# A graph layer on one core: 62 row tiles for 58, ScalarE's addresses at column 64, and the first receivers' copy behind the table's last write

## The chip, the cores and the metric

The kernel runs on one core of one Trainium2 chip. The metric is the device time of one execution in microseconds (us), as the median over runs. The engines are named as in the profile: PE is TensorE, DVE is VectorE, ACT is ScalarE, POOL is GpSimd and SP is SyncE; ACTq and SPq are the instruction queues of ScalarE and SyncE, which also issue DMA transfers, and PEld is TensorE's loading of weights.

## The reference

One layer of a graph network: 6250 nodes with 128 features, 206250 edges sorted by receiver. For each edge two small networks give a weight vector, the sender's key and value are fetched, and a weighted sum goes to the receiver; a residual and a layer norm follow.

```python
w_ij = silu(edge_feats @ rad_W1 + rad_b1) @ rad_W2 + rad_b2
w_ij = w_ij + silu(chi_scalar @ sph_W1 + sph_b1) @ sph_W2 + sph_b2
q_i = (x @ Wq).reshape(-1, 8, 16)[receivers]
k_j = (x @ Wk).reshape(-1, 8, 16)[senders]
alpha = (q_i * w_ij.reshape(-1, 8, 16) * k_j).sum(-1) / sqrt(16) * cutoffs[:, None]
v_j = (x @ Wv)[senders].reshape(-1, 8, 16)
out = segment_sum(alpha[..., None] * v_j, receivers) / 16
return layernorm(x + out.reshape(-1, 128))
```

## The kernel before

**Tiles.** Edges are cut into 403 *quads* of 512 edges (four tiles of 128, one edge a partition), four quads to a *group*, two groups to a pair. The list `order` holds the quads in the sequence of processing. The loop runs over groups g and four slots; i counts its passes, and pass i multiplies quad i+1, while activations are made one quad further ahead.

**Table phase (up to about 57 us).** The node features come in by 13 chunks. TensorE turns each chunk and multiplies it with Wk and Wv (L392), VectorE copies the product out (L394), and SyncE writes it to the table `kv_tab` in DRAM (L399): one row of 1 KB, key and value, for each node. The first 8 quads get their keys and values from gathered node features by the same matmuls instead of from the table (`gather_x`, tile `msg`). Beside this the receivers of each edge, relative to a group's first node, are turned (L472), written to DRAM as `rel_lin` (L480), copied within DRAM to `rel_pair`, repeated four times (L488), and read back as `relb` (L272), from which VectorE makes the one-hot matrices `hotT` (L301). For the first group this is `first_rel`, which stands beside chunk 7; for all others it is `store_rel(1, PAIRS)` behind the table phase. SyncE's queue runs in order, so what stands behind a waiting DMA there waits too.

**Gathers.** From quad 8 on, keys and values come from `kv_tab`. GpSimd issues one indirect DMA for each 128 edges (L141), 14 quads ahead of their use, into a ring of 16 buffers. The first of them needs the whole table written.

**Row tiles.** In some quads the last of the four tiles is not gathered by GpSimd. Its 128 rows are fetched by 128 plain DMAs of 1 KB (L210) into `wide`, issued by SyncE and ScalarE. ROW_TILES is their number, spread evenly over passes 8 to 401; ROW_ACT is the number of rows of each that ScalarE issues, the others are SyncE's. An address has to stand in a register of the issuing engine, and loads from the tile `at_i` put it there (L204, TENSOR_LOAD): 32 registers at a time on SyncE and 24 on ScalarE (ROW_UNITS). `at_i` is made once, by VectorE's copies of a turned list (L811 and L812). How many rows an engine issues in a pass is dealt out by `load_rows` from the pass number; a load counts as six rows. ScalarE issues one row at each of two places between its activations and the rest at the end of the pass.

**A quad's arithmetic.** First layers on TensorE (L566), SiLU on ScalarE (L603, two a quad), second layers (L618), queries at edges (L585); VectorE multiplies by the keys (L634, which waits for the gathers and rows in its queue at L631) and by the weights (L642), sums by head (L644), scales (L647) and forms messages (L659); TensorE sums the messages with one-hot matrices (L670, L711). SiLU of a quad waits for a mark of TensorE, and TensorE's first layers wait for SiLU to free one of two PSUM banks.

## Time and profile before

| | |
|---|---|
| median of 3 runs | 1966.89 us (1962.34 to 1968.69) |
| the profiled execution | 1962.43 us, span 1960.5 us |
| mean granted TensorE clock | 0.955 |
| gathers of keys and values on GpSimd (L141) | 1522 |
| rows issued by ScalarE and SyncE (L210) | 4176 and 3248 |
| loads of addresses, ScalarE and SyncE (L204) | 174 and 116 |
| busy share of the DMA engines in most slices | 0.5 |

In the profile's rows a number of partitions and elements stands behind the tile names, "x" is a count, and "|" parts busy time and mean from the idle time before the group and what ended it. In the answers by source line, min/median/max of the duration in ns follow the count, then the first and the last start in us. In the order of time, a row begins with start and length in us. Windows give busy us and counts of PE, PEld, DVE, ACT and POOL, then the granted clock, the share of the DMA engines and GB/s.

### The profile page before, as it was taken

The numbers are of one execution on the slowest core, as the hardware profiler recorded it, in microseconds if no ns is written. First come the engines' busy times: TensorE is split into PE (matmuls) and PEld (weight loads), VectorE is DVE, ScalarE is ACT, GpSimd is POOL, SyncE is SP. The second block draws the span as 40 slices with busy tenths as digits, with TensorE's granted clock in tenths as the row PEclk, the third lists the DMA queues.
The fourth block names the chain that finished last, engine by engine and source line by source line (L and its number), as shares of the span: only waits on it lengthen the run. The fifth ranks groups of instructions, "written<-read, shape, count | busy, mean of one in ns | idle before, by whom it ended". The sixth has DMA issues, their size and how long they took to land.

```text
span 1960.5 us, 55953 instructions
## 1 busy us (share of the span) xinstructions
PE 1785.3 (91%) x16005; PEld 1498.5 (76%) x16005; DVE 1521.0 (78%) x3366; ACT 644.3 (33%) x1361; POOL 1471.3 (75%) x1562
## 2 busy tenths in 40 slices
PE   9999999998999999888988899989899898988888
PEld 7777777777877777777877777777777777777777
DVE  6787888778887787777777777877777777777778
ACT  3333333332333333333333333333333333323234
POOL 7777777777777777777777777777777777777775
PEclk9999999998999999989989999999899999999999
DMA  9755555555555555555545554555555555545543
GB/s 324 222 144 147 166 145 164 152 145 150 166 144 151 168 145 149 165 143 152 168 142 146 161 155 144 147 168 145 145 150 166 143 145 161 155 142 148 163 133 99
DMA packets 148925, 307.13 MB, mean 157 GB/s; under 512 B 40326, under 2 KB 76608, under 8 KB 148608
## 3 DMA queue, kind: packets, MB, share of 16 engines
q0 software_dynamic: 74080, 201.69, 36.8%
q1 hardware_dynamic: 64400, 96.98, 15.2%
q10 hardware_dynamic: 10128, 4.82, 1.2%
q8 instruction: 127, 2.08, 0.4%
q14 instruction: 190, 1.56, 0.3%
HBM read 289.88 MB, written 15.11 MB: 156 GB/s over the span
## 4 chain that ended last, share of the span: by engine, by line
ACTq 24%; POOL 16%; DMA 16%; DVE 14%; issue 13%; PE 10%; ACT 3%; POOLq 0%; DVEq 0%
ACTq L210 19%; POOL kv L141 16%; DMA kv<-kv_tab,src_i 16%; ACTq L204 5%; PE pw L618 4%; DVE kq L634 3%; DVE side L644 2%; PE pq L585 2%; DVE kq L642 2%; ACT act L603 2%; DVE msg L659 2%; PE ph L566 2%; PE po L670 1%; DVE side L647 1%; PE pq L711 0%
## 5 line engine op out<-in xcount | busy, mean ns | idle before, releaser
L141 POOL DMA_INDIRECT kv<-kv_tab,src_i x1522 | 1439.7, 946 | 465.5 <-issue 395.4
L603 ACT ACTIVATE act<-ph,b 128x512 f32<-128x512 f32 x806 | 554.5, 689 | 1265.6 <-issue 752.0
L618 PE MATMUL pw<-w,act 128*128 128x128 f32 x6448 | 875.0, 292 | 0.0
L618 PEld LDWEIGHTS pw<-w,act 128*128 128x128 f32 x6448 | 796.3, 201 | 52.8 <-issue 7.7
L566 PE MATMUL ph<-feats,w 32*128 32x512 f32 x1612 | 600.0, 665 | 54.3 <-ACT act L603 51.5
L634 DVE TENSOR_TENSOR kq<-pq,kv 128x512 f32<-128x512 f32 (+1 forms) x404 | 270.6, 670 | 358.3 <-DVEq L631 197.3
L585 PE MATMUL pq<-q,hotT 32*128 32x128 f32 x3224 | 490.0, 292 | 5.9 <-DVE kq L634 5.8
L585 PEld LDWEIGHTS pq<-q,hotT 32*128 32x128 f32 x3224 | 408.6, 193 | 26.0 <-DVE kq L634 21.3
L566 PEld LDWEIGHTS ph<-feats,w 32*128 32x128 f32 x1612 | 180.6, 188 | 206.2 <-ACT act L603 149.9
L644 DVE TENSOR_REDUCE side<-kq 128x32 f32<-128x512 f32 x404 | 280.3, 694 | 14.0
L659 DVE TENSOR_TENSOR msg<-kv,side 128x512 f32<-128x512 f32 (+1 forms) x404 | 269.1, 666 | 13.9
L642 DVE TENSOR_TENSOR kq<-pw,kq 128x512 f32<-128x512 f32 x404 | 274.6, 680 | 0.0
L573 PE MATMUL pw<-brow,onesb 3*128 3x512 bf16 x403 | 158.2, 393 | 0.0
L670 PE MATMUL po<-msg,hot 128*32 128x128 f32 x3200 | 153.6, 289 | 0.0
L711 PE MATMUL pq<-part,to 128*128 128x128 f32 x196 | 45.2, 314 | 77.5 <-DVE kq L634 77.5
L670 PEld LDWEIGHTS po<-msg,hot 128*32 128x32 f32 x3200 | 71.1, 110 | 37.9 <-issue 3.8
L711 PEld LDWEIGHTS pq<-part,to 128*128 128x128 f32 x196 | 31.1, 200 | 87.5 <-DVE kq L634 79.2
L647 DVE TENSOR_TENSOR side<-side,scale 128x32 f32<-128x32 f32 x400 | 79.8, 199 | 13.7
L301 DVE TENSOR_TENSOR hotT<-relb,side 128x512 f32<-128x512 bf16 x101 | 68.7, 681 | 1.5 <-DMA relb<-rel_pair 1.5
L306 DVE TENSOR_TENSOR hot<-rel,side 128x512 f32<-128x512 f32 x100 | 68.0, 680 | 0.0
L295 PE MATMUL pq<-wq,xT 128*128 128x128 f32 x200 | 43.0, 298 | 25.9 <-DVE kq L634 25.7
L295 PEld LDWEIGHTS pq<-wq,xT 128*128 128x128 f32 x200 | 31.0, 195 | 31.8 <-DVE kq L634 28.0
(133 smaller groups left out, 824.9 us busy)
## 6 DMA issues: line engine op xcount, KB each, us to landing
wide<-kv_tab ACTq DMA_DIRECT2D x4176, 1.0 KB
wide<-kv_tab SPq DMA_DIRECT2D x3248, 1.0 KB
feats<-in_edges SPq DMA_DIRECT2D x50, 1024.0 KB
kv<-kv_tab,src_i POOLq DMA_INDIRECT x1522, 3.2
relb<-rel_pair SPq DMA_DIRECT2D x50, 256.0 KB
x<-in_x SPq DMA_DIRECT2D x101, 64.0 KB
out<-y SPq DMA_DIRECT2D x101, 64.0 KB
kv_tab<-kv SPq DMA_DIRECT2D x12, 512.0 KB
```

The source lines that it names most:

```text
L141: return nc.gpsimd.indirect_dma_start(out=o, out_offset=None, in_=table, in_offset=bass.IndirectOffsetOnAxis(ap=index, axis=0))
L210: o = engine.dma_start(row_of[q][p:p + 1, 0, :].bitcast(U8), table[:, ds(regs.pop(p), ROW_BYTES)])
L566: return nc.tensor.matmul(act_of[q, i], w1[r0:r0 + R, :], feats_of[g][r0:r0 + R, c0:c0 + EQ], start=True, stop=True)
L573: nc.tensor.matmul(pw, onesb[f:f + 3, :], brow[f:f + 3].rearrange("p t d -> p (t d)"), start=True, stop=False)
L585: o = nc.tensor.matmul(pq_of[q][:, t, :], hotT_of[g][b, t * P:(t + 1) * P], q_of[g][b, :], start=True, stop=True)
L603: o = nc.scalar.activation(act, act_of[q, i], AF.Silu, bias=b1[:, i:i + 1])
L618: o = nc.tensor.matmul(pw[:, t, :], act_of[q, i][:, t * P:(t + 1) * P], w2[:, i, :], start=False, stop=(t == QT - 1 and i == 1))
L634: o = nc.vector.tensor_tensor(kq_of[q][:, u, :], pq_of[q][:, u, :], kv[:, :, :D], op=OP.mult)
L642: nc.vector.tensor_tensor(m, pw_of[q][:, t, :], m, op=OP.mult)
L644: nc.vector.tensor_reduce(alpha, m.rearrange("p t (h e) -> p t h e", e=HD), AX.X, OP.add)
L659: nc.vector.tensor_tensor(msg_of[q][:, u, :].rearrange("p t (h e) -> p t h e", e=HD), kv[:, :, D:].rearrange("p t (h e) -> p t h e", e=HD) ...
L670: o = nc.tensor.matmul(po_of[g][j * W:(j + 1) * W, :], hot_of[g][:, j * QT + t, :], msg_of[g * NQ + j][:, t, :], start=(t == 0), stop=(t = ...
```

## The change

The number of row tiles goes from 58 to 62. In each, ScalarE issues 70 rows instead of 72 and SyncE 58 instead of 56. In `at_i` the addresses no longer stand at their row's number: SyncE's begin at column 0 and ScalarE's at column 64, so the tile is 144 columns wide and VectorE fills it with four copies instead of two. Further, the copy from `rel_lin` to `rel_pair` becomes a function of its own, `store_pairs`; for the first group it is called behind the last write of `kv_tab`, in the last chunk's pass, no longer beside chunk 7. For the other groups it stays directly behind `store_rel`.

```diff
--- before.py
+++ after.py
@@ -49,11 +49,12 @@
 MSGS = 10
 ACTS = 8
 RING = 16
-ROW_TILES = 58
+ROW_TILES = 62
 ROW_FIRST = 8
 ROW_LAST = 401
 ROW_LEAD = 6
-ROW_ACT = 72
+ROW_ACT = 70
+ROW_AT = {SP: 0, ACT: 64}
 ROW_LOAD = 6
 ROW_CARRY = 2
 ROW_UNITS = {SP: 32, ACT: 24}
@@ -201,8 +202,9 @@
             regs = {}
 
             def load(e, m):
+                c = ROW_AT[name] + e - a
                 regs.update(zip(range(e, e + m), nc.values_load_multi_w_load_instructions(
-                    at_i[q % P:q % P + 1, q // P, e:e + m], engines=(name,), min_val=0,
+                    at_i[q % P:q % P + 1, q // P, c:c + m], engines=(name,), min_val=0,
                     max_val=(N - 1) * ROW_BYTES,
                     skip_runtime_bounds_check_because="senders are nodes")[1]))
 
@@ -480,6 +482,9 @@
                     nc.sync.dma_start(
                         rel_lin[h, u:e:NQ].rearrange("n m e -> m n e"),
                         relT[p:p + GT, u // NQ:u // NQ + n, :])
+        def store_pairs(c, d):
+
+            ends_at = [min(d, (NG + 1 - h) // 2) for h in range(2)]
             for h, e in enumerate(ends_at):
                 r = rel_lin[h].rearrange("u (j t) e -> (u j) (t e)", t=QT)
                 m = e - (e - c) % NQ
@@ -544,6 +549,7 @@
             for f in beside.get(k, []):
                 f()
             if i == len(chunks) - 1:
+                store_pairs(0, 1)
                 load_rel(0, gp, 1)
                 load_feats(0)
                 for g in range(1, XL):
@@ -554,6 +560,7 @@
             gathers(q, mark_of[quads_x[n + 2 + (n > 1)], "x"] if n else None)
         nc.vector.tensor_tensor(bsum, b2[:, 0:1], b2[:, 1:2], op=OP.add)
         store_rel(1, PAIRS)
+        store_pairs(1, PAIRS)
         nc.vector.tensor_scalar(scale, scale, SCALE, None, op0=OP.mult)
 
 
@@ -800,7 +807,7 @@
             nc.vector.tensor_scalar(general, found, 0.0, None, op0=OP.is_gt)
 
         rows_f = quad_of("kq", 3).rearrange("p t d -> p (t d)")[:, :QUADS]
-        at_i = lp.tile([P, math.ceil(QUADS / P), P], I32, name="at_i")
+        at_i = lp.tile([P, math.ceil(QUADS / P), ROW_AT[ACT] + 80], I32, name="at_i")
 
         def turn_rows():
             pt = pp.tile([P, EQ], F32, name="pq", bufs=2).rearrange("p (t d) -> p t d", d=P)
@@ -808,8 +815,10 @@
             for i in range(full + 1):
                 n = min(P, QUADS - i * P)
                 nc.tensor.transpose(pt[:n, i, :], rows_f[:, i * P:i * P + n], ident)
-            nc.vector.tensor_copy(at_i[:, :full, :], pt[:, :full, :])
-            nc.vector.tensor_copy(at_i[:n, full, :], pt[:n, full, :])
+            m = P - ROW_ACT
+            for a, b, at in ((0, m, ROW_AT[SP]), (m, P, ROW_AT[ACT])):
+                nc.vector.tensor_copy(at_i[:, :full, at:at + b - a], pt[:, :full, a:b])
+                nc.vector.tensor_copy(at_i[:n, full, at:at + b - a], pt[:n, full, a:b])
 
         written, ready, ready_at = [], [], []
         load_rel(1, lp, 2)
```

The change moves lines, so the listings of the changed program below have L482, L493, L401, L274, L258 for L480, L488, L399, L272, L256, and L212, L206, L610, L292, L722 for L210, L204, L603, L290, L715. On SyncE, at the end of the table phase, where the last writes of the table and the first group's receivers meet, this stands before:

```order
L399 DMA kv_tab<-kv 128x1024
L480 DMA rel_lin<-relT 16x128 x2
L488 DMA rel_pair<-rel_lin 16x1x512 x2
L399 DMA kv_tab<-kv 128x1024 x4
L399 DMA kv_tab<-kv 128x256
L272 DMA relb<-rel_pair 128x1x1024
L256 DMA feats<-in_edges 128x2x1024
```

and this with the change:

```order
L401 DMA kv_tab<-kv 128x1024
L482 DMA rel_lin<-relT 16x128 x2
L401 DMA kv_tab<-kv 128x1024 x4
L401 DMA kv_tab<-kv 128x256
L493 DMA rel_pair<-rel_lin 16x1x512 x2
L274 DMA relb<-rel_pair 128x1x1024
L258 DMA feats<-in_edges 128x2x1024
```

The two copies to `rel_pair` have moved behind the five last table writes and stand directly ahead of the load of `relb` that reads them; the load of `feats` still follows that.

On ScalarE, in the third and fourth pass with rows, between activations (`act`, `xT`, `tot`), before:

```order
L603 ACTIVATE act_102<-ph,b_72 128x512
L210 DMA wide<-kv_tab 1x1024
L290 ACTIVATE xT<-pq 128x128
L603 ACTIVATE act_103<-ph,b_72 128x512
L210 DMA wide<-kv_tab 1x1024 x11
L603 ACTIVATE act_104<-ph,b_72 128x512
L210 DMA wide<-kv_tab 1x1024
L715 ACTIVATE tot<-pq 128x128
L210 DMA wide<-kv_tab 1x1024
L603 ACTIVATE act_105<-ph,b_72 128x512
L210 DMA wide<-kv_tab 1x1024 x10
L204 TENSOR_LOAD at_i
```

and with the change, about the same place:

```order
L292 ACTIVATE xT<-pq 128x128
L212 DMA wide<-kv_tab 1x1024
L610 ACTIVATE act_103<-ph,b_72 128x512
L212 DMA wide<-kv_tab 1x1024 x12
L610 ACTIVATE act_104<-ph,b_72 128x512
L212 DMA wide<-kv_tab 1x1024
L722 ACTIVATE tot<-pq 128x128
L212 DMA wide<-kv_tab 1x1024
L610 ACTIVATE act_105<-ph,b_72 128x512
L212 DMA wide<-kv_tab 1x1024 x4
L206 TENSOR_LOAD at_i
```

A stretch between two quads' activations now takes 12 rows where it took 10 or 11, and the loads come after fewer quads.

On VectorE the four casts that fill `at_i` stand where two stood, between the first quad's message and the second quad's multiply, and the four new row tiles split eight operations in two. TensorE's sequence is the same, and GpSimd issues 1518 gathers instead of 1522.

## The prediction

> **What bounds the kernel now.** I read the page first, then GpSimd's order of time, then counts by line in windows, then ScalarE's queue.
>
> ```profile
> PE 1785.3 (91%) x16005; PEld 1498.5 (76%) x16005; DVE 1521.0 (78%) x3366; ACT 644.3 (33%) x1361; POOL 1471.3 (75%) x1562
> L141 POOL DMA_INDIRECT kv<-kv_tab,src_i x1522 | 1439.7, 946 | 465.5 <-issue 395.4
> ...
> 44.45 0.94 POOL L141 DMA_INDIRECT kv<-kv_tab,src_i  x1 [1.42 <-DVE kv L394]
> 45.70 0.95 POOL L141 DMA_INDIRECT kv<-kv_tab,src_i  x1 [0.30 <-issue]
> ...
> 1947.23 0.95 POOL L141 DMA_INDIRECT kv<-kv_tab,src_i  x1 [0.30 <-issue]
> ```
>
> TensorE has the largest share, yet GpSimd is the engine without a pause. From the first gather's start to the last one's there are 1521 steps in 1902.8 us, 1.251 us each, and a neighbouring pair shows the same step: 0.95 busy and 0.30 to issue. A quad takes four gathers, one fewer where a row tile replaces one, so with 58 tiles over 393 quads GpSimd's pace is (4 - 58/393) x 1.251 = 4.819 us a quad.
>
> That sets the end only while someone waits for it. I count gathers issued (L141) and first multiplies started (L634, one a quad) up to four moments:
>
> ```profile
> L141 POOL DMA_INDIRECT kv<-kv_tab,src_i x45: 942/946/1221, 44.4 to 99.8; - x45
> L634 DVE TENSOR_TENSOR kq<-pq,kv x10: 668/692/693, 59.2 to 98.7; 128x512 f32<-128x512 f32 x10
> ...
> L141 POOL DMA_INDIRECT kv<-kv_tab,src_i x276: 942/946/1221, 44.4 to 388.8; - x138
> L634 DVE TENSOR_TENSOR kq<-pq,kv x73: 550/692/693, 59.2 to 384.6; 128x512 f32<-128x512 f32 x64, 128x384 f32<-128x384 f32 x9
> ...
> L141 POOL DMA_INDIRECT kv<-kv_tab,src_i x556: 942/946/1221, 44.4 to 739.0; - x186
> L634 DVE TENSOR_TENSOR kq<-pq,kv x150: 549/692/693, 59.2 to 738.9; 128x512 f32<-128x512 f32 x130, 128x384 f32<-128x384 f32 x20
> ...
> L141 POOL DMA_INDIRECT kv<-kv_tab,src_i x1484: 942/946/1221, 44.4 to 1899.7; - x186
> L634 DVE TENSOR_TENSOR kq<-pq,kv x391: 547/692/694, 59.2 to 1895.0; 128x512 f32<-128x512 f32 x168, 128x384 f32<-128x384 f32 x28
> ```
>
> The first 8 quads need no gather and a row quad needs three. At 100 us ten multiplies have used 8 gathers of 45: 37 are ahead. At 390 it is 276 - (65 x 4 - 9) = 25, at 740 it is 556 - (142 x 4 - 20) = 8, at 1900 again 1484 - (383 x 4 - 56) = 8. So there are two regimes: until about 740 the arithmetic runs faster than GpSimd and eats its head start of 29 gathers (36.3 us); after that it waits for each gather to land. The waits agree: in 100 to 390 us VectorE's multiply waits for TensorE, in 850 to 1900 for its own queue's wait on the landings.
>
> ```profile
> DVE kq L634 <- PE pq L585: 45.1, 48, 2.3
> ...
> DVE kq L634 <- DVEq L631: 180.8, 119, 3.9
> ```
>
> What sets the pace of the first regime? ScalarE's engine is only a third busy, but its queue also issues row transfers. Here are 100 to 390 us (L603 twice a quad), then ten row issues in a stretch:
>
> ```profile
> L603 ACT ACTIVATE act<-ph,b x128: 682/688/692, 100.8 to 388.5; 128x512 f32<-128x512 f32 x128
> L210 ACTq DMA_DIRECT2D wide<-kv_tab x678: 227/228/538, 100.8 to 389.7; - x170
> L204 ACTq TENSOR_LOAD <-at_i x29: 1707/1810/1954, 98.7 to 385.8; - x29
> ...
> 105.69 3.10 ACTq L210 DMA_DIRECT2D wide<-kv_tab  x10
> ...
> PEld ph L566 <- ACT act L603: 44.5, 82, 1.9
> ```
>
> 64 quads in 290 us are 4.53 us a quad. A row costs (3.10 - 0.23)/9 = 0.32 us of the queue, a load 1.81 and about 0.06 around it. 678 rows and 29 loads make 217 + 54 = 271 of the 290 us; the 19 left are 0.3 us a quad for dispatching activations. The queue is full, and TensorE's weight loads wait for its SiLUs. So the first regime is bound by ScalarE's instruction queue, at 4.53 us a quad.
>
> **The change part by part.** *Four gathers fewer.* 4 x 1.251 = 5.0 us off GpSimd; its pace becomes (4 - 62/393) x 1.251 = 4.807.
>
> *The receivers' copy moved.* The startup on SyncE and its two readers:
>
> ```profile
> 29.23 1.66 SPq L480 DMA_DIRECT2D rel_lin<-relT  x2
> 34.04 1.48 SPq L488 DMA_DIRECT2D rel_pair<-rel_lin  x2
> 35.61 4.26 SPq L399 DMA_DIRECT2D kv_tab<-kv  x5
> 39.97 1.36 SPq L272 DMA_DIRECT2D relb<-rel_pair  x1
> ...
> 45.48 0.69 DVE L301 TENSOR_TENSOR hotT<-relb,side 128x512 f32<-128x512 bf16 x1 [1.52 <-DMA relb<-rel_pair]
> ```
>
> The copy waits 3.1 us (30.89 to 34.04) for its input to land, with five table writes queued behind. Without it the last write is issued about 2 us earlier, when its data is ready. The first gather then starts up to 1.42 - 0.30 = 1.1 us earlier; GpSimd's gathers of x keep it from more. I take 1.1 (bounds 0 and 1.1). Now the relb load, with feats, x and scale behind it, waits for the copy: issue about 37.8 to 39.3, plus a landing like those 3.1 us, so relb leaves at 42.4 instead of 39.97. VectorE already idles 1.52 us for it and the table-phase copies stand behind. Compute starts 0 to 2.4 us later; I take 2, since the wait is exposed.
>
> *More rows on ScalarE.* Rows per quad go from 58 x 72/393 = 10.63 to 62 x 70/393 = 11.04: +0.42 x 0.32 = 0.133 us. Loads go from 174/393 to 186/393: +0.03 x 1.87 = 0.057. Every third load fetches 22 registers instead of 24; SyncE's loads of 24 and 32 registers span
>
> ```profile
> L204 SPq TENSOR_LOAD <-at_i x116: 1673/1960/2302, 73.5 to 1902.0; - x116
> ```
>
> so at most 0.08 us a register, -0.02 a quad. What starting at column 64 does for a load is unshown. It lies between all loads at the fastest (1.71 instead of 1.81: -0.05 a quad) and at the slowest (1.95: +0.07). ScalarE's loads began at three columns (56, 80, 104) and hardly vary, so I take 0. The queue needs 4.53 + 0.133 + 0.057 - 0.02 = 4.70 us a quad, bounds 4.65 to 4.77.
>
> *More on the others.* SyncE gets 348 rows (111 us) and 8 loads, covered by 332 us that it waits for marks of TensorE; uncovered, rows would come late and add to VectorE's L631 wait.
>
> ```profile
> SPq L324 <- PE pq L585: 218.4, 73, 10.1
> SPq L256 <- PE pq L585: 113.9, 45, 4.6
> ```
>
> VectorE gets two small casts once and eight operations split in two (550 + 281 ns for 692), under its 22% of idle time; uncovered, some 2 us.
>
> ```profile
> L634 DVE TENSOR_TENSOR kq<-pq,wide 128x128 f32<-128x128 f32 x58 | 16.3, 281 | 0.0
> ```
>
> *Clock.* The quiet pace is not the mean. Windows 100 to 390, 390 to 500, 500 to 740, 850 to 1900, with granted clock after the counts:
>
> ```profile
> 100.00:390.00 290.00, 269.65 (x2483) 221.20 (x2483) 232.77 (x513) 97.51 (x205) 219.24 (x232) 1.00 0.53 154
> 390.00:500.00 110.00, 100.81 (x916) 86.33 (x914) 90.19 (x204) 35.40 (x75) 83.19 (x88) 0.91 0.53 153
> 500.00:740.00 240.00, 226.20 (x2067) 186.27 (x2067) 194.78 (x435) 82.03 (x173) 181.59 (x192) 0.99 0.53 152
> 850.00:1900.00 1050.00, 947.21 (x8566) 799.19 (x8565) 802.00 (x1770) 338.47 (x716) 793.75 (x841) 0.94 0.53 152
> ...
> L603 ACT ACTIVATE act<-ph,b x46: 682/688/694, 390.9 to 496.8; 128x512 f32<-128x512 f32 x46
> ```
>
> At 0.91 a quad took 110/23 = 4.78 us, 0.25 more. From 100 to 740 the clock was 0.98 and 140 quads took 4.573 each, 0.04 over the quiet pace. A slower ScalarE leaves TensorE idle more often, so I take 0.06: compute at 4.76 us a quad, bounds 4.74 (that mean) and 4.87 (clock 0.94 throughout: 0.06/0.09 x 0.25 = 0.17).
>
> *The sum.* The head start to lose is 36.3 + 1.1 (earlier gathers) + 2 (later compute) + 2 (0.17 us on some 12 quads before 100 us) = 41.4 us. The last 8 quads carry no rows and run faster:
>
> ```profile
> 1930.37 0.69 DVE L634 TENSOR_TENSOR kq<-pq,kv 128x512 f32<-128x512 f32 x1
> 1934.38 0.68 DVE L634 TENSOR_TENSOR kq<-pq,kv 128x512 f32<-128x512 f32 x1
> 1937.86 0.68 DVE L634 TENSOR_TENSOR kq<-pq,kv 128x512 f32<-128x512 f32 x1
> 1941.59 0.69 DVE L634 TENSOR_TENSOR kq<-pq,kv 128x512 f32<-128x512 f32 x1
> ```
>
> that is 3.74 each, and win 8 x 1.07 = 8.5. The other 33 must be lost over 384 quads, 0.086 a quad, so compute has to do 4.72 to catch GpSimd. At 4.76 it wins 384 x 0.047 = 18 and ends 15 us behind. GpSimd's own end moves by -5.0 - 1.1 = -6.1. Sum: +9 us on the span 1960.5, on this execution's 1962.43 (1.9 us lie outside the span): 1971. The median of the runs, 1966.89, is 4.5 above that execution; I forecast 1976.
>
> **The rivals.** *A: compute still catches up and GpSimd sets the end.* Then it is 6.1 us faster, 1961. For it: quiet compute at 4.70 is under 4.72. Against: that margin is 0.02, half of what the clock already cost before 740 us.
>
> *B: the clock falls and stays low.* TensorE idles in more stretches, runs them at half rate, and its late marks hold ScalarE back. At 4.87 compute loses 384 x 0.063 = 24 instead of winning: 33 + 24 - 6 = +51, 2018. For it: the window with most idle time (850 on, TensorE 90% busy) has 0.94. Against: 100 to 390 kept 1.00 at 93%. The Trainium skill, "TensorE: Matmul & The Clock Gate", Part 1, says that the clock goes to half after an idle window of about 3.4 us and returns after a busy one; the rows of lower clock where TensorE waits fit that, and by this rule alone the change tends towards B.
>
> *C: the copy gives back all it gains and nothing else moves.* If row issues hid in ScalarE's waits, rows would be free and the end would be -5 to -6, within noise of A. The full queue of 100 to 390 us speaks against it; I count it with A.
>
> **How the numbers follow.** A measurement tells about 0.3% (5.9 us) from no change. Compute-bound, 4.73 to 4.82 a quad (-2 to +32 us): 0.6, of it 0.48 above +5.9. A with C: 0.28, half of it beyond -5.9. B: 0.12. So faster 0.18, same 0.22, slower 0.60. The likeliest's own range is 1965 to 1999; with A it reaches down to 1960: 1960 to 1999.
>
> **What would show it.** The same count of gathers ahead should fall from some 38 at 100 us to clearly above 8 at the end, and the L634 wait on L631 should almost vanish. SiLU pairs should be 4.7 or more apart, relb's wait at L301 some 2 us longer, the first gather near 43.3. If the head start is gone by 1500 us, or ScalarE's loads are much shorter from column 64, the forecast is wrong on the fast side; a mean clock under 0.95 says B.

## The result and the profile after

| | before | after |
|---|---|---|
| median of the runs | 1967.07 us (1962.34 to 1968.69, 4 runs) | 2028.62 us (2025.04 to 2031.87, 4 runs) |
| span of the profiled execution | 1960.5 us | 2023.2 us |
| mean granted TensorE clock | 0.955 | 0.953 |

The changed kernel is slower: the ratio is 1.031, with a 95% interval of 1.0294 to 1.0326. The direction was forecast, the size was not: 9 us were forecast, 62 came.

Three parts of the changed kernel's profile: busy times, then the chain that ended last by engine and by line, then the gathers.

```profile
PE 1851.2 (91%) x16005; PEld 1525.8 (75%) x16005; DVE 1522.9 (75%) x3376; ACT 645.3 (32%) x1361; POOL 1471.5 (73%) x1558
...
ACTq 62%; issue 14%; PE 12%; ACT 7%; DVE 4%; DMA 0%; SPq 0%; DVEq 0%
ACTq L212 49%; ACTq L206 13%; ACT act L610 5%; PE pw L625 4%; PE ph L573 3%; PE pq L592 2%; PE pk L394 1%; DVE kq L641 1%; DVE side L651 1%; DVE kq L649 1%; PE po L677 1%; ACT y L753 1%; PE pt L384 0%; ACT q L299 0%; ACT part L713 0%
...
L142 POOL DMA_INDIRECT kv<-kv_tab,src_i x1518 | 1439.6, 948 | 471.9 <-issue 394.5
```

GpSimd's work is hardly changed, and nothing that GpSimd does is in the chain any more. ScalarE's queue alone makes 62% of it, 49% by row issues (L212) and 13% by loads of addresses (L206). Before, that chain was mixed:

```profile
ACTq 24%; POOL 16%; DMA 16%; DVE 14%; issue 13%; PE 10%; ACT 3%; POOLq 0%; DVEq 0%
```

The waits between 850 and 1900 us of the changed kernel (the stretch in which before's multiply waited for landed gathers, 180.8 us of it) agree:

```profile
ACT act L610 <- issue: 642.1, 189, 5.5
DVE kq L641 <- PE pq L592: 226.0, 180, 4.1
...
PEld ph L573 <- ACT act L610: 192.0, 315, 2.8
```

No wait of the multiply for a landing is left. TensorE waits for SiLUs, VectorE for TensorE, and a SiLU mostly for no other engine (71 us for TensorE stand against the 642): it stands behind row issues and loads in ScalarE's own queue. Now gathers issued (L142) and first multiplies (L641), as the prediction counted them, up to 100, 390, 740 and 1900 us:

```profile
L142 POOL DMA_INDIRECT kv<-kv_tab,src_i x44: 942/949/1440, 44.9 to 99.4; - x44
L641 DVE TENSOR_TENSOR kq<-pq,kv x9: 669/691/692, 60.8 to 95.6; 128x512 f32<-128x512 f32 x9
...
L142 POOL DMA_INDIRECT kv<-kv_tab,src_i x275: 942/949/1440, 44.9 to 388.8; - x138
L641 DVE TENSOR_TENSOR kq<-pq,kv x69: 550/692/693, 60.8 to 385.4; 128x512 f32<-128x512 f32 x60, 128x384 f32<-128x384 f32 x9
...
L142 POOL DMA_INDIRECT kv<-kv_tab,src_i x555: 942/949/1440, 44.9 to 739.9; - x185
L641 DVE TENSOR_TENSOR kq<-pq,kv x141: 546/692/693, 60.8 to 736.1; 128x512 f32<-128x512 f32 x121, 128x384 f32<-128x384 f32 x20
...
L142 POOL DMA_INDIRECT kv<-kv_tab,src_i x1475: 941/949/1440, 44.9 to 1900.0; - x185
L641 DVE TENSOR_TENSOR kq<-pq,kv x378: 545/692/693, 60.8 to 1896.0; 128x512 f32<-128x512 f32 x160, 128x384 f32<-128x384 f32 x29
```

Gathers ahead are 44 - 4 = 40 at 100 us, 275 - (61 x 4 - 9) = 40 at 390, 555 - (133 x 4 - 20) = 43 at 740 and 1475 - (370 x 4 - 58) = 53 at 1900. Before they fell from 37 to 8. The arithmetic never catches GpSimd; it falls further behind until GpSimd is held: 53 gathers at 3.84 a quad are about the 14 quads that it may run ahead.

From 100 to 1900 us before starts 391 - 10 = 381 multiplies, after 378 - 9 = 369: 1800/381 = 4.72 us a quad and 1800/369 = 4.88. Some 384 quads at 0.154 us more are 59 us, and the first multiply is 1.6 us later (60.8 for 59.2). Together that is 61 of the 62.7 us on the span.

To see what fills ScalarE's queue, I summed every record of it within a window and divided by the quads (half the number of L610 SiLUs). "Each" is the mean of a row's issue with the 29 ns move before it; "gaps" is the time between records, on the right the gaps in which a SiLU is dispatched, where waiting shows too.

```
us a quad           window    quad  rows   each   rows  loads  gaps  gaps at SiLUs
before              100-390   4.53  10.59  273 ns 2.89  0.79   0.64  0.19
before              850-1900  4.78  10.61  271 ns 2.88  0.80   0.64  0.47
after               100-390   4.83  11.00  276 ns 3.04  0.88   0.68  0.21
after               850-1900  4.90  11.07  281 ns 3.11  0.89   0.68  0.21
```

Before, the queue waits in the second stretch (0.47) and works through in the first (0.19). After, it works through everywhere.

### The profile page after: what moved, and what is told of

Same layout as the page of the kernel before. It is cut to its first block, busy times and chain, and to the rows that moved or that the text cites. A ratio compares the mean times of both kernels' runs of the same rounds, so it can differ in the third digit from the quotient of the medians.

```text
span 2023.2 us, 57021 instructions
## 1 busy us (share of the span) xinstructions
PE 1851.2 (91%) x16005; PEld 1525.8 (75%) x16005; DVE 1522.9 (75%) x3376; ACT 645.3 (32%) x1361; POOL 1471.5 (73%) x1558
## 4 chain that ended last, share of the span: by engine, by line
ACTq 62%; issue 14%; PE 12%; ACT 7%; DVE 4%; DMA 0%; SPq 0%; DVEq 0%
ACTq L212 49%; ACTq L206 13%; ACT act L610 5%; PE pw L625 4%; PE ph L573 3%; PE pq L592 2%; PE pk L394 1%; DVE kq L641 1%; DVE side L651 1%; DVE kq L649 1%; PE po L677 1%; ACT y L753 1%; PE pt L384 0%; ACT q L299 0%; ACT part L713 0%
## 5 line engine op out<-in xcount | busy, mean ns | idle before, releaser
L142 POOL DMA_INDIRECT kv<-kv_tab,src_i x1518 | 1439.6, 948 | 471.9 <-issue 394.5
L610 ACT ACTIVATE act<-ph,b 128x512 f32<-128x512 f32 x806 | 554.4, 689 | 1325.8 <-issue 1155.7
L625 PE MATMUL pw<-w,act 128*128 128x128 f32 x6448 | 892.3, 296 | 0.0
L625 PEld LDWEIGHTS pw<-w,act 128*128 128x128 f32 x6448 | 812.4, 205 | 52.0 <-issue 5.9
L573 PE MATMUL ph<-feats,w 32*128 32x512 f32 x1612 | 691.2, 653 | 151.1 <-ACT act L610 145.7
L641 DVE TENSOR_TENSOR kq<-pq,kv 128x512 f32<-128x512 f32 (+1 forms) x404 | 270.2, 669 | 416.4 <-PE pq L592 400.9
L573 PEld LDWEIGHTS ph<-feats,w 32*128 32x128 f32 x1612 | 212.9, 186 | 374.9 <-ACT act L610 345.6
L592 PE MATMUL pq<-q,hotT 32*128 32x128 f32 x3224 | 477.1, 288 | 0.0
L592 PEld LDWEIGHTS pq<-q,hotT 32*128 32x128 f32 x3224 | 399.3, 191 | 0.6 <-issue 0.5
L753 ACT ACTIVATE y<-y,shift,rs 128x128 f32<-128x128 f32 x98 | 48.6, 496 | 0.0
L394 PE MATMUL pk<-wkv,xT 128*128 128x256 f32 x162 | 40.1, 389 | 3.2 <-DVE kv L396 3.2
```

The lines of the kernel that those rows point to most:

```text
L142: return nc.gpsimd.indirect_dma_start(out=o, out_offset=None, in_=table, in_offset=bass.IndirectOffsetOnAxis(ap=index, axis=0))
L573: return nc.tensor.matmul(act_of[q, i], w1[r0:r0 + R, :], feats_of[g][r0:r0 + R, c0:c0 + EQ], start=True, stop=True)
L592: o = nc.tensor.matmul(pq_of[q][:, t, :], hotT_of[g][b, t * P:(t + 1) * P], q_of[g][b, :], start=True, stop=True)
L610: o = nc.scalar.activation(act, act_of[q, i], AF.Silu, bias=b1[:, i:i + 1])
L625: o = nc.tensor.matmul(pw[:, t, :], act_of[q, i][:, t * P:(t + 1) * P], w2[:, i, :], start=False, stop=(t == QT - 1 and i == 1))
L641: o = nc.vector.tensor_tensor(kq_of[q][:, u, :], pq_of[q][:, u, :], kv[:, :, :D], op=OP.mult)
```

## Experiments

Each kernel ran against before on the same chip. "us a quad" is 1800 us over the multiplies that begin between 100 and 1900 us. All rows but the last two ran beside a before of 1964.75 to 1968.70 us, the last two beside 1965.17.

| run | what differs | median us | ratio (95%) | us a quad |
|---|---|---|---|---|
| after | the change | 2028.62 | 1.031 (1.0294 to 1.0326) | 4.88 |
| moved_copy | before, the copy moved | 1965.21 | 0.9997 (0.9982 to 1.0013) | |
| tiles62_act72 | before, 62 tiles | 2024.39 | 1.0298 (1.0282 to 1.0313) | 4.88 |
| tiles62_act64 | after, 64 rows on each queue | 2013.08 | 1.0238 (1.022 to 1.0255) | 4.85 |
| padded_loads | after, odd loads begun earlier | 2216.99 | 1.1284 (1.1261 to 1.1307) | |
| loads_of_24 | after, odd loads ended later | 2025.71 | 1.0293 (1.0276 to 1.031) | 4.85 |
| scalar_from_58 | after, column 58 | 2469.33 | one run | |
| sync_rows_in_one | after, SyncE's rows in one transfer | 2005.75 | 1.02 (1.018 to 1.022) | 4.77 |
| scalar_rows_in_one | after, ScalarE's rows in one transfer | 1962.89 | 0.9975 (0.9964 to 0.9985) | 4.72 |
| one_load_fourth | after, one load a tile on ScalarE | 2008.61 | 1.0221 (1.0204 to 1.0238) | 4.85 |
| tiles60_act72_fourth | before, 60 tiles | 1979.91 | 1.0089 (1.0068 to 1.011) | 4.74 |

**Which part of the change does it.** First, only the receivers' copy moved, in before:

```diff
+        def store_pairs(c, d):
...
+                store_pairs(0, 1)
```

> The kernel before with the receivers' copy moved alone (58 tiles, 72 rows on ScalarE, old columns). Theory Q (ScalarE's instruction queue sets the end of the changed kernel): the copy costs a later start of compute, some 2 us, which the gathers hide at 58 tiles; 1965 to 1969 us, no change. Rival M (the moved copy is a main cause): 1985 us or more.

The copy alone changes nothing that can be measured (0.9982 to 1.0013). Second, before with the number of tiles alone:

```diff
-ROW_TILES = 58
+ROW_TILES = 62
```

> The kernel before with 62 row tiles alone (72 rows on ScalarE at the old columns, the copy in its old place, all loads of 24 or 32 registers). Theory Q: ScalarE's rows per quad rise from 11.04 to 11.36 against the changed kernel (+0.32 x 0.30 = +0.10 us a quad, 384 quads: +37), its third load is back at 1.80 instead of 2.02 us (-14): 2045 to 2060 us. Rival L (the odd load sizes of 22 and 26 registers are the main cause): 2000 us or less. Rival M: 1970 us or less.

This run has nearly all of the loss: 60 of 62 us, at the same 4.88 us a quad, with the addresses where before has them. So the copy, the columns and the split of 70 and 58 are together, as a net, worth no more than a few us, and the four tiles are worth the rest. The 2045 to 2060 expected by theory Q were missed: 72 rows a tile made 11.38 rows a quad on ScalarE instead of 11.07, but they took 275 ns each instead of 281, so the rows cost nearly the same (3.13 for 3.11 us a quad, in the table further down). So a row has no fixed price.

**Is it ScalarE's queue?** ScalarE's 70 row issues of a tile became one transfer of 70 consecutive rows, without its loads:

```diff
+                    o = engine.dma_start(row_of[q][a:b, 0, :], kv_tab[a:b, :])
```

> After, with the 70 single-row transfers that ScalarE issues for each row tile replaced by one transfer of 70 consecutive table rows, and ScalarE's register loads left out (so these rows are not the gathered ones, and the output is not the reference's); SyncE's 58 rows a tile are as in after. Theory Q (ScalarE's instruction queue, filled by row issues and loads, is what sets the end of after): the queue has some 4 us a quad less to do, VectorE's first multiply waits for the landed gathers again, and GpSimd sets the end: 1957 to 1965. Rival T (with 62 tiles TensorE, its clock or VectorE's eight-way split pieces set the pace, and ScalarE's full queue is a follower): the kernel stays above 2000.

Theory Q held. The chain of that run by engine, then its waits:

```profile
DVE 26%; POOL 24%; DMA 22%; PE 14%; issue 12%; SPq 0%; DVEq 0%; POOLq 0%; another core or an unknown queue 0%; ACT 0%
```

```profile
ACT act L622 <- PE pq L604: 1225.3, 389, 9.4
...
DVE kq L653 <- DVEq L650: 314.3, 205, 4.0
```

The SiLUs now wait for TensorE and the first multiply for landed gathers: GpSimd sets the end, 4.9 us under before (0.0025 x 1968.7; 3 to 7 by the interval). That is what four gathers fewer were said to be worth, 5.0 us. TensorE and VectorE do the same work as in after and keep up with GpSimd, so they are not what made after slower. The edit takes away more than issues, though: 4340 one-row transfers are gone as well. What tells the queue from the transfers is that in after no multiply waits for a landing, and the next run.

**Does SyncE's issuing slow ScalarE's?** The same edit on SyncE's 58 rows instead:

> After, with the 58 single-row transfers that SyncE issues for each row tile replaced by one transfer of 58 consecutive table rows, and SyncE's register loads left out (so these rows are not the gathered ones, and the output is not the reference's); ScalarE's 70 rows a tile are as in after. Theory K (the two queues slow each other: in before and after a row issue on ScalarE averages 243 and 251 ns, and many last over 300): without SyncE's 3596 row issues ScalarE's rows take some 0.02 to 0.03 us less each, 11 a quad, so its queue needs 4.9 - 0.2 to 0.3 = 4.6 to 4.7 us a quad, under GpSimd's 4.807, and the kernel ends at 1960 to 1990. Rival L (a row issue costs ScalarE the same whatever SyncE does): the queue stays at 4.85 to 4.9 us a quad and the kernel at 2020 to 2030. In both SyncE's queue is nearly empty, which by itself changes nothing, since it waited for marks of TensorE already.

In part: the end lies between the two forecasts. All records from 100 to 1900 us, the row's issue alone, without the move:

```
                   ScalarE: rows  mean ns  over 300 ns   SyncE: rows  mean ns  over 300 ns
before                      4062  243      248                  3164  237      109
after                       4076  251      440                  3391  244      231
sync_rows_in_one            4163  241      226                     -    -        -
```

The sums of ScalarE's queue from 850 to 1900 us, for this kernel and for others that follow:

```
us a quad               quad  rows   each   rows  loads  gaps  gaps at SiLUs
after                   4.90  11.07  281 ns 3.11  0.89   0.68  0.21
tiles62_act72           4.88  11.38  275 ns 3.13  0.85   0.69  0.21
sync_rows_in_one        4.77  11.03  270 ns 2.98  0.89   0.68  0.23
loads_of_24             4.88  11.06  284 ns 3.14  0.86   0.68  0.20
one_load_fourth         4.88  11.04  281 ns 3.10  0.29   0.68  0.81
tiles60_act72_fourth    4.74  10.98  276 ns 3.03  0.82   0.67  0.22
```

With SyncE's issues gone, ScalarE's row falls from 251 to 241 ns (with its move 281 to 270), and the queue from 4.90 to 4.77 us a quad. In after alone, a row issue of ScalarE that overlaps a DMA issue of SyncE takes 255 ns on average (2899 of them), the others 242. So the two queues do slow each other. In this profile that is 0.12 us a quad; but it is of the fastest execution (1991.65), and by the medians (2028.62 to 2005.75) it is 23 us, some 0.06 a quad. K expected 0.02 to 0.03 us a row and an end under 1990, and got 0.011 and 2005.75. Even alone, ScalarE's queue needs at least 4.77 us a quad, more than the 4.72 at which compute can still catch GpSimd: the number of rows and the loads do that by themselves. The Trainium skill, "Perfetto Trace Analysis", section "DMA Instruction — HWDGE (DVE, Sync)", says that the block that writes the descriptors is shared by the two issuing sequencers and locked by one at a time, and that the duration in a profile includes the wait for the lock. The 10 ns here, and the 13 ns of overlapping issues, agree in kind.

**Fewer rows on ScalarE.** After with the rows split 64 and 64:

```diff
-ROW_ACT = 70
+ROW_ACT = 64
```

> The changed kernel with 64 rows of each tile on ScalarE and 64 on SyncE (loads of 24, 24, 16 and of 32, 32). Theory Q: ScalarE's queue does 10.10 rows a quad, fewer than before the change (10.63), so compute catches the gathers again and GpSimd sets the end: 1960 to 1964 us. Rival R (the larger number of rows itself, by transfers or waits for them, slows the gathers or VectorE): stays above 2000 us. If SyncE's queue overflows, VectorE's wait on the landings grows and the time lies between.

Theory Q fell, and the third case of the expectation came: ScalarE's queue got its slack, and only some 15 us came back (2013.08 for 2028.62). The chain by engine, then the waits:

```profile
SPq 23%; ACTq 19%; DMA 19%; PE 15%; issue 10%; DVE 7%; ACT 3%; DVEq 0%
```

```profile
ACT act L610 <- PE pq L592: 443.3, 120, 14.2
...
DVE kq L641 <- DVEq L638: 203.1, 33, 11.9
```

Now the multiply waits 203 us in 33 pieces for landings, up to 11.9 us each. They are not GpSimd's gathers, but SyncE's rows ("DMA wide<-kv_tab" makes 19% of the chain by line). SyncE's queue is full in its turn: its 208 us of waits for marks of TensorE in after (L326, L258) are down to a few.

**Is a queue the plain sum of what is in it?** Two edits of ScalarE's loads, first the third load of a tile lengthened from 22 to 24 registers (SyncE's second goes from 26 to 32, and `at_i` is set to zero before it is filled):

```diff
+                n = m + -m % 8
...
-                    at_i[q % P:q % P + 1, q // P, c:c + m], engines=(name,), min_val=0,
+                    at_i[q % P:q % P + 1, q // P, c:c + n], engines=(name,), min_val=0,
```

> After, with each register load lengthened at its end to a multiple of eight registers (22 to 24 on ScalarE, 26 to 32 on SyncE; the extra registers are not used, every load starts where it did). ScalarE's third load of a tile took 2.02 us with 22 registers, its loads of 24 took 1.80. Theory R (a load is dear when its count is not a multiple of eight): 62 x 0.22 = 14 us come back, since ScalarE's queue is full: 2011 to 2018. Rival S (the third load is dear for its place, whatever it fetches): no change, 2025 to 2030. With SyncE nothing changes by either, since its load of 32 takes 2.19 us and that of 26 2.18.

The load did what R said: the mean of every third load fell from 2.02 to 1.81 us. The end did what S said: 1.0293, within the interval of after. By the table loads went from 0.89 to 0.86 us a quad and rows from 3.11 to 3.14. Some 13 us were taken from the queue and about 3 came back. Whether the rows took up the rest, or runs on another chip differ by so much, these runs don't tell.

Then two of three loads were left out, and with them the slow first row behind each:

```diff
+                if name == ACT and e > a:
+                    regs.update((p, kept[(p - a) % ROW_UNITS[name]]) for p in range(e, e + m))
+                    return
```

> The kernel of one_load_a_tile once more, since so far the kernel before itself took 2500 us and more in its groups. (Rows 24 to 69 of ScalarE's 70 reuse the registers of the first load, so they are repeats.) Theory Q (ScalarE's queue is a plain sum of what is in it): 4.9 - 0.7 = 4.2 us a quad, GpSimd sets the end, 1957 to 1966. Rival P (what both queues issue together is limited, and time freed comes back as longer row issues): a row issue on ScalarE grows from 251 ns to some 280, the queue stays at 4.75 us a quad or more, the end at 1980 to 2025.

Both theories fell, each in another half. ScalarE's queue did come free, as Q said: its loads take 0.29 us a quad instead of 0.89, its rows the same 281 ns, and the gaps at SiLUs grow from 0.21 to 0.81 us, which is waiting. So the mechanism of P (ScalarE's issues get longer) isn't there. But the end is at 2008.61, as P said, and not at 1960. Its chain by line, its longest wait of the multiply (205 us for landings again, in 38 pieces), and SyncE's row issues of this run and of after (min/median/max ns):

```profile
DMA wide<-kv_tab 25%; ACTq L217 14%; SPq L217 12%; PE pw L630 9%; PE pq L597 5%; PE ph L578 5%; DVE kq L646 2%; PE po L682 2%; ACT act L615 2%; ACTq L210 2%; PE pk L399 1%; SPq L210 1%; DVE side L656 1%; PE pq L723 1%; DVE kq L654 1%
```

```profile
DVE kq L646 <- DVEq L643: 205.2, 38, 10.5
```

```profile
L217 SPq DMA_DIRECT2D wide<-kv_tab x3398: 224/228/3388, 100.0 to 1899.8; - x200
```

```profile
L212 SPq DMA_DIRECT2D wide<-kv_tab x3392: 224/228/592, 99.9 to 1899.8; - x200
```

SyncE issues the same rows, but some of them now take up to 3.4 us where none took over 0.6, and their mean goes from 244 to 302 ns. A piece of SyncE's queue in order of time, then of the chain of the same run:

```profile
1249.37 0.41 SPq L263 DMA_DIRECT2D feats<-in_edges  x1
1249.88 5.92 SPq L217 DMA_DIRECT2D wide<-kv_tab  x5
...
1260.55 18.16 SPq L217 DMA_DIRECT2D wide<-kv_tab  x27
```

```profile
1270.49 0.23 SPq L217
1270.82 14.85 DMA wide<-kv_tab
1285.99 0.76 DVE kq L646 x2
```

Five rows take 5.92 us right behind the load of the next pair's edge features (1 MB), and for a row issued about 1270.5 the chain counts 14.85 us until the multiply can go on. Of the SyncE issues of over 0.6 us in this run, 188 of 189 lie within 20 us behind a feature load. In after SyncE issues rows there too, and none is slow. The DMA packets in the traces show what differs. Below, the k-th row issue of a queue is matched with that queue's k-th packet of 1 KB; of each feature load, which is 256 packets of 4 KB, stand the start of the 240th and of the last (medians from 100 to 1800 us, in us after the issue; the last column counts from 100 to 1900):

```
                     ScalarE's rows  SyncE's rows  feature load: 240th   last  SyncE issues over 0.6 us
before                         3.9           4.1                   4.5    6.4           1
tiles62_act72                  6.1           6.6                   4.7   10.1           0
after                          7.1           7.9                   4.9   11.0           0
loads_of_24                    7.6           9.1                   4.8   12.6           6
tiles62_act64                  7.8          10.6                   5.0   14.9          66
one_load_fourth                9.7          13.4                   4.8   17.7         189
scalar_rows_in_one               -           1.1                   4.4    5.0           1
sync_rows_in_one               1.2             -                   4.3    4.8           -
```

Of every feature load one sixteenth, 16 packets, comes late, and the later, the later the rows come. These 16 and the rows of both queues also run one at a time (98% of the time in which any of them runs in after, 99% in one_load_fourth), while of the first 240 some 15 run at once for half of the time. So the one-row transfers of both queues seem to share one of the 16 DMA engines with a sixteenth of everything else; the trace names no engine, so that is inferred. By an estimate from the packets' durations (all rows and the 4-byte packets of both queues, and a sixteenth of the rest) that engine is busy 0.88 of the time in before, 0.94 in after and 0.96 in one_load_fourth, where the mean over all engines is about 0.5. In after a row is late by 7 to 8 us and no multiply waits for it; in one_load_fourth and tiles62_act64 it is later than the multiply can bear. That SyncE's slow issues come from the same backlog is likely, since they grow with it, but not shown. The Trainium skill, "DMA: Bandwidth & Descriptors", section "Issuing engines are not separate DMA queues", says that what ScalarE, SyncE and GpSimd start runs on the same 16 DMA engines and interleaves; rows of both queues that grow late together fit it.

So there are two limits close together at 62 tiles. ScalarE's queue needs at least 4.77 us a quad by itself and 4.88 beside SyncE's; with ScalarE's relieved, SyncE's rows land late and the pace is 4.85. In sync_rows_in_one the rows' path is free (1.2 us) and the pace is still 4.77, so in after it is the queue that binds.

**Where does it begin?** Before with 60 tiles:

> The kernel of tiles60_act72 once more, for the same reason: before with 60 row tiles instead of 58. Theory Q: 4.71 to 4.80 us a quad where compute is not waiting, so 1962 if it catches GpSimd at the last, up to 1990 if not. Rival U (the step from 58 to 62 tiles is even, 15 us a tile): 1995 to 2000.

Theory Q held and U fell: two tiles cost 17 us (0.0089 x 1965), the next two, by tiles62_act72, 41. At 60 tiles the queue is full already (4.74 us a quad, gaps at SiLUs 0.22), just above the 4.72 that compute has to do. Before sits at the edge, and no kernel here that computes the reference beats it by more than a measurement tells.

Another 60-tile version, 68 rows a tile on ScalarE with loads of 24 and 32 registers, was meant to:

> After with 60 tiles instead of 62 and 68 rows a tile on ScalarE instead of 70, every load lengthened at its end to a multiple of eight registers (so ScalarE's are of 24, SyncE's of 32). ScalarE then issues 4080 rows, 96 fewer than in before, with 6 loads more; SyncE issues 3600, as many as in after. Theory Q (ScalarE's own queue sets the pace): 4.53 - 0.07 + 0.03 = 4.5 us a quad, compute catches GpSimd as in before, and two gathers fewer end it at 1962 to 1966, at best a match with or a little under before. Rival P (the two queues together are limited at some 0.24 us a row): 7680 rows need 4.73 us a quad, and the end is 1968 to 1985.

It has no reading. That run and those that follow here fell in groups where before itself took 2500 to 2531 us, with TensorE and both queues pausing for no recorded reason, so that something else set the end. The tries of one load a tile and of 60 tiles before the two that were read above, each with its median and that of before beside it:

> After, with one register load a tile on ScalarE instead of three: rows 24 to 69 of its 70 reuse the first load's 24 registers, so these rows are repeats and the output is not the reference's. Row issues keep their form and number. 124 loads of 1.8 to 2.0 us and the slow first row behind each (0.47 us instead of 0.23) leave ScalarE's queue: 124 x 2.2 = 270 us, 0.69 us a quad. Theory Q (the queue is a plain sum of what is in it): 4.9 - 0.7 = 4.2 us a quad, so GpSimd sets the end again, 1957 to 1966. Rival P (what both queues can issue together is limited, and time freed in one comes back as longer row issues, as it seemed when the third load was shortened): the mean row issue on ScalarE grows from 251 ns to some 280, the queue stays full at 4.75 us a quad or more, and the end at 1980 to 2025.

2593.02 us (before 2530.68).

> Before with 60 row tiles instead of 58, all else as before (ScalarE 72 rows a tile, three loads of 24). Theory Q (compute has to do 4.72 us a quad to catch GpSimd; before's queue does 4.53 in its quiet stretch, two tiles add 2 x 72/393 x 0.27 + 6/393 x 1.87 = 0.13, and slower row issues some 0.05): 4.71 to 4.80, so 1962 if it catches up at the last, up to 1990 if not. Rival U (the step from 58 to 62 tiles is spread evenly, 15 us a tile): 1995 to 2000.

2535.23 us (before 2530.68); tiles60_act68 in the same group took 2571.42. In the next group:

> The kernel of one_load_a_tile once more, since in that group of runs the kernel before itself took 2531 us, with TensorE pausing between matrix multiplies. (Rows 24 to 69 of ScalarE's 70 reuse the registers of the first load, so they are repeats.) Theory Q (ScalarE's queue is a plain sum of what is in it): 4.9 - 0.7 = 4.2 us a quad, GpSimd sets the end, 1957 to 1966. Rival P (what both queues issue together is limited, and time freed comes back as longer row issues): a row issue on ScalarE grows from 251 ns to some 280, the queue stays at 4.75 us a quad or more, the end at 1980 to 2025.

2595.22 us (before 2530.10).

> The kernel of tiles60_act72 once more, for the same reason: before with 60 row tiles instead of 58. Theory Q: 4.71 to 4.80 us a quad where compute is not waiting, so 1962 if it catches GpSimd at the last, up to 1990 if not. Rival U (the step from 58 to 62 tiles is even, 15 us a tile): 1995 to 2000.

2534.41 us (before 2530.10).

> The kernel of tiles60_act68 once more, for the same reason: after with 60 tiles, 68 rows a tile on ScalarE, loads lengthened to 24 and 32 registers. Theory Q (ScalarE's own queue sets the pace): 4.5 us a quad, compute catches GpSimd as in before, and two gathers fewer end it at 1962 to 1966. Rival P (both queues together are limited at some 0.24 us a row): 7680 rows need 4.73 us a quad, the end at 1968 to 1985.

2567.63 us (before 2530.10). And in a third:

> The kernel of one_load_a_tile a third time, since in both groups so far the kernel before itself took 2530 us. (Rows 24 to 69 of ScalarE's 70 reuse the registers of the first load, so they are repeats.) Theory Q (ScalarE's queue is a plain sum of what is in it): 4.9 - 0.7 = 4.2 us a quad, GpSimd sets the end, 1957 to 1966. Rival P (what both queues issue together is limited, and time freed comes back as longer row issues): a row issue on ScalarE grows from 251 ns to some 280, the queue stays at 4.75 us a quad or more, the end at 1980 to 2025.

2545.62 us (before 2500.02).

> The kernel of tiles60_act72 a third time, for the same reason: before with 60 row tiles instead of 58. Theory Q: 4.71 to 4.80 us a quad where compute is not waiting, so 1962 if it catches GpSimd at the last, up to 1990 if not. Rival U (the step from 58 to 62 tiles is even, 15 us a tile): 1995 to 2000.

2505.27 us (before 2500.02). None of these says anything of theories Q, P and U, since ScalarE's queue was not what set the end; so whether 60 tiles with 68 rows would beat before stays open.

**The columns.** Two runs put loads at other addresses. One begins each odd load a few columns earlier, so that it has a multiple of eight registers:

```diff
+                n = -m % 8
-                c = ROW_AT[name] + e - a
+                c = ROW_AT[name] + e - a - n
```

> The changed kernel with its odd loads (22 registers on ScalarE, 26 on SyncE) begun earlier, so that they fetch 24 and 32 registers; the surplus is not used. Theory Q with the load sizes as one term: ScalarE's third load falls from 2.02 to 1.80 us, 62 x 0.22 = 14 us less on a queue that is always full: 2013 to 2018 us. If load sizes do not matter: 2028 us. Rival L: 1985 us or less.

The other sets ScalarE's addresses right behind SyncE's:

```diff
-ROW_AT = {SP: 0, ACT: 64}
+ROW_AT = {SP: 0, ACT: 58}
```

> After with ScalarE's addresses from column 58 on, right behind SyncE's 58, instead of from column 64. Theory A (a load whose first byte is not at a multiple of 32 takes some three times as long, as the 5.6 us instead of 2.0 and the 6.9 instead of 2.2 of the loads begun at columns 110 and 26 showed): ScalarE's three loads begin at columns 58, 82 and 106 and take 5 to 6 us each instead of 1.8 to 2.0, which adds 186 x 3.3 to 4 = 610 to 740 us to a full queue: 2640 to 2770. Rival B (what made those loads slow was their reading across the end of the other engine's addresses, or their count): the loads stay near 2 us and the kernel at 2028.

In the first, the loads begun at columns 110 and 26 took up to 5.7 and 7.1 us instead of 2.0 and 2.2:

```profile
L207 ACTq TENSOR_LOAD <-at_i x26: 1691/1824/5682, 99.9 to 384.7; - x26
L207 SPq TENSOR_LOAD <-at_i x17: 2071/2337/7079, 108.8 to 374.1; - x17
```

In the second, who is slow changes with time. Windows 100 to 390, 850 to 1300 and 1570 to 1900 us:

```profile
L206 ACTq TENSOR_LOAD <-at_i x21: 5024/5487/5673, 103.8 to 376.2; - x21
L206 SPq TENSOR_LOAD <-at_i x15: 2106/2196/2328, 101.3 to 385.4; - x15
...
L206 ACTq TENSOR_LOAD <-at_i x41: 1672/1838/2160, 852.4 to 1299.9; - x41
L206 SPq TENSOR_LOAD <-at_i x26: 5537/6317/7154, 852.3 to 1291.2; - x26
...
L206 ACTq TENSOR_LOAD <-at_i x24: 4933/5506/5689, 1577.6 to 1890.4; - x24
L206 SPq TENSOR_LOAD <-at_i x17: 2120/2181/2302, 1579.8 to 1892.3; - x17
```

The bytes sort it, if the tile itself begins at a multiple of 16. With 58, a row of `at_i` for 128 quads has 138 addresses of 4 bytes, 552 bytes. In the first row SyncE starts at byte 0 and ScalarE at 232, in the second at 552 and 784, in the third at 1104 and 1336. The fast starts (0, 784, 1104) are multiples of 16, the slow ones (232, 552, 1336) are 8 over; so are columns 110 and 26 of the first run (bytes 440 and 104). Theory A was right that the start makes it, wrong that ScalarE's loads are slow throughout, and so 2469 us instead of 2640 to 2770. Column 64 avoids this, with rows of 576 bytes; column 56, where before has them, avoids it as well.

## Why the prediction was right and wrong

**What bounds the kernel: right.** Two paces, GpSimd's and that of ScalarE's queue, and the later one sets the end: scalar_rows_in_one takes one away and gets the other. The break-even of 4.72 us a quad is where tiles60_act72_fourth (4.74) begins to lose.

**Four gathers fewer, -5.0 us: right,** and of no use, since GpSimd no longer sets the end.

**The receivers' copy, -1.1 and +2 us: right in moved_copy, and too small for the end to tell.** There GpSimd's wait before the first gather falls from 1.42 to 0.30 us, which is the 1.1 (the first gather starts at 43.7 instead of 44.4). The load of `relb` leaves at 42.28 (42.4 forecast), and the first multiply starts 1.8 us later (61.0 for 59.2). But tiles62_act72, with the copy in its old place, has its first multiply at 61.0 too, so runs differ by as much. In the profile of after SyncE's startup is about 1.5 us late already ahead of the moved copy (L482 at 30.68 for 29.23), and the first gather starts at 44.9.

**"At 4.76 it wins 384 x 0.047 = 18": the step that failed.** The pace of compute was built as 4.53 + 0.133 + 0.057 - 0.02 + 0.06. From the table (after 850 to 1900 against before 100 to 390), term by term:

| term | forecast | measured |
|---|---|---|
| rows and the gaps around them | +0.133 | (3.11 - 2.89) + (0.68 - 0.64) = +0.26 |
| loads | +0.057 - 0.02 | 0.89 - 0.79 = +0.10 |
| clock, TensorE's late marks | +0.06 | 0.21 - 0.19 = +0.02 |
| sum | +0.23 | +0.38 |

*Rows.* The number was right (11.04 forecast, 11.07 measured). The price was taken as fixed at 0.32 us; it rose from 273 to 281 ns plus gaps. Without SyncE's issues it is 270 (sync_rows_in_one), so most of that rise goes with the other queue's issues. A price that is measured while two queues compete is a price for that load of both.

*Loads.* The number was right; the -0.02 had the wrong sign. It took a load to cost so much a register, but 22 registers take 2.02 us and 24 take 1.80: +0.22 x 62/393 = +0.035 a quad. That column 64 does nothing to aligned loads was right: the first two take 1.80 and 1.82, as before.

*Clock.* Taken as 0.06 with bounds up to 0.17. The mean stays (0.953 for 0.955), but the compute-bound stretch of 100 to 390 us had 1.00 before and has 0.95 after (100 to 740 us: 0.98 and 0.95):

```profile
100.00:390.00 290.00, 265.96 (x2343) 218.97 (x2341) 219.66 (x486) 91.23 (x193) 219.22 (x232) 0.95 0.52 148
```

So the clock did fall where compute sets the pace, as rival B said, but it costs little there: the gaps at SiLUs, in which late marks would show, grew by 0.02 us a quad and not by 0.06 to 0.17. B came closest in its figure (2018) for a price that didn't occur. The Trainium skill, "TensorE: Matmul & The Clock Gate", Part 1, pointed towards B; here TensorE waits in more, but short, pieces (192.0 us in 315, none over 2.8 us), and the mean clock stays.

With 4.88 in place of 4.76 the prediction's own sum gives 33 + 384 x (4.88 - 4.807) - 6 = 55 us on the span, where 62.7 were measured. One more reading was off: the last eight quads were taken as 3.74 us each from four rows, but all eight steps of before's trace take 34 us (1919.4 to 1953.4), 4.25 each, so they win back about 4.5 us and not 8.5, and the sum becomes 59. The mechanism was right, and the sizes of the pace's terms were not. The bounds of that pace, 4.74 to 4.87, took in the clock, and a row's price only as it stood before.

**The rivals.** A (compute still catches up, 1961) and C (row issues hide) fell: the multiply's wait on landings is gone, and the queue has no slack.

**What would show it.** Gathers ahead were to start near 38 and stay clearly above 8: 40, and they rose to 53. L634's wait on landings was to vanish: it did. SiLU pairs were to be 4.7 apart or more: 4.83 to 4.90. The mean clock under 0.95 that would have spoken for B: 0.953. The first gather near 43.3 and relb's wait 2 us longer did not come (44.88; 1.6 us for 1.5).

## What to carry to other kernels

Where two engines' paces lie within a few per cent, an edit that trades work of one for work of the other is judged by the slower pace after it, and the bounds of a forecast must take in the price of each unit as the load grows, not only the number of units. A queue that looks idle by its engine's busy share (ScalarE 32%) can be full, and a queue that looks free because it waits for marks (SyncE) can become the bound when the other one is relieved, so balance is tried by taking the work off each queue in turn. And a mean over 16 DMA engines (0.5 here) says little where many small transfers go one at a time: compare when the first and the last packets of a large transfer start.

## What the hardware showed unexpectedly

- A load of registers from SBUF depends on where it begins: 1.8 to 2.2 us for 22 to 32 registers from a byte that is a multiple of 16, 5 to 7 us from one that is 8 over (padded_loads and scalar_from_58, if the tile itself begins at a multiple of 16).
- It is not proportional to its count: 24 registers 1.80 us, 22 registers 2.02, 32 registers 2.19, 26 registers 2.18 (means over all records of after and before). Lengthened from 22 to 24, the same load took 1.81.
- The first row behind a load takes about twice the 0.23 us of the others to issue. From the chain of one_load_fourth, a load (L210) and the row behind it:

```profile
1207.81 1.84 ACTq L210
1209.82 0.47 ACTq L217
```

- One-row transfers issued by SyncE within 20 us of a 1 MB load took up to 3.4 us to issue in one_load_fourth (3.9 in tiles62_act64), and their packets started 13.4 us after the issue in the median (7.9 in after).
- One-row transfers of two queues run one at a time, and a sixteenth of each large transfer waits among them: in after 240 of a feature load's 256 packets have started 4.9 us after the issue and the last one at 11.0 us; when one of the two queues sends its rows in one transfer, all 256 have started within 5 us (medians).
